# Block products for q and v in the attention layers of a four-layer graph network, with new step orders

## The chip, the cores and the metric

The kernel runs on one core of a Trainium2 chip. The metric is the device time of one execution in microseconds (us), as the median of several runs; lower is better.

## The reference

The input is x with 128 graphs of 64 nodes and 256 channels, 8192 rows in all, and one 64 x 64 adjacency matrix. Four layers follow one another, each with a residual:

```
h = relu(layernorm(x));  x = x + layer(h)
layer 0: normalized adjacency, two linear maps with batch norms
layer 1: two graph convolutions, then LSTMs over windows of 1 to 4 nodes
layer 2: q, k, v = split(h @ Wqkv); softmax(q k^T / 16 + adj, causal) v @ Wo
layer 3: q, k, v of 4 heads of 64 channels; softmax(q k^T / 8, masked where adj == 0) v
```

Everything is float32. This case is about layers 2 and 3. The kernel folds the weights of layer 2 beforehand: `wg0_sb` holds the product of the q and k weights, so that the scores are (h wg0) h^T and no k is computed, and `wg1_sb` holds the product of the v and output weights. So layer 2 has two projections of 256 x 256, layer 3 has three.

## The kernel before, in words

**Chunks.** The rows are cut into 16 chunks (`NCH`) of 512 rows (`CH`), four tiles (`NJ`) of 128 rows each. x stays in SBUF the whole time, one tile `xs[c]` a chunk. For a projection the kernel wants h with channels on the partitions (`hT`, two blocks `k` of 128 channels, 512 columns of rows). Most chunks get it by transposing 32 x 32 squares on VectorE, writing the result to DRAM (`put`) and reading it back with permuted rows (`get`, four transfers); a few use TensorE transposes (`chan2`, `chan3`).

**Attention as steps.** The part after the LSTMs is a list of small functions, the steps. Four order strings name them, with a chunk offset: `q2+0` is step q2 for the running chunk, `qa-2` is qa for the chunk two before. The order is written out by hand, and each engine executes its instructions of all steps in exactly this order. So a step that waits on an engine holds everything that is queued behind it there, on SP's queue of transfers too. FIRST opens the stage, THIRD does chunk 3, ROUND is the steady chunk, NORM a steady chunk that also prepares layer-2 input for chunks 14 and 15, LAST ends it. The offsets make the layers overlap: while chunk c is in layer 2, chunk c-2 has its layer-3 projections and chunk c-3 its last products.

The steps that the text speaks of:

- `load2`: reads hT of layer 2. `q2`, `copyq2`: q = two times two matmuls of 512 columns (`project_t`, L1526), copied from PSUM by ScalarE and VectorE. `v2a`, `v2b`: v, eight matmuls of 256 columns (`project_v`, L1519), two copies on ScalarE.
- `score2` (L1719): scores, then mask and maximum on VectorE, subtraction on GpSimd; `exp2` on ScalarE; `divide2` on VectorE; `turn2`: TensorE transposes (L1662); `out2` (L1750): product with v, added to x by VectorE (L1753).
- `keep`, `back`: write x to DRAM and read it in another order. `norm3a`, `norm3b`: statistics on VectorE, 1/sqrt on GpSimd. `apply3`: normalize and relu on ScalarE. `square3`: transposes on VectorE and the write. `load3`: the read.
- `sums_h` (GpSimd), `qa`, `q5`, `c11`, `q6`, `q3`, `c12`, `qc`, `qd`: q and k of layer 3 with seven block products (L1826), below. `v3a`, `v3b`: v of layer 3, as v2a and v2b. `q30`, `k30`, `q31`, `k31`: the plain projections, used for chunks 0 and 15 (before: for chunk 0 of the opening and the last chunk).
- `score3`, `exp3`, `sum3`, `divide3`, `turn3`, `out3` and `store`: the softmax of layer 3, its product and the write of the result. The last chunk has it in halves (`score3h`, `exp3a`, `turn3a`, `out3a`, `storea` and so on).
- `res1`, `pair1`: the layer-1 residual of chunks 14 and 15 and the reordering of their x, in the opening.

**Seven products.** A product of 2 x 2 blocks can be had with seven block products in place of eight, if sums of blocks are formed beforehand. For q and k of layer 3 the kernel does that: `sums_w` forms the sums of weight blocks once, `sums_h` the sums of blocks of hT for each chunk (four operations of 128 x 256 on GpSimd), `seven` issues the products into three PSUM banks X, Y, Z that go on accumulating, and copies (ScalarE) and adds (VectorE) take the four result blocks out at the right moments. X holds products 1, 6, 7 and 4 in turn, so that each has to wait until the sum before it has been read.

**PSUM.** In this stage eight banks are handed out in turn; the ninth request waits until the first bank has been read.

Of the kernel before, what the change touches and what calls it, by code (L numbers as in the profile page):

```python
# [13 lines left out]
P = 128  # L14
# [5 lines left out]
def kernel(  # L20
# [1508 lines left out]

    def begin_attention():  # L1530

        tiles = [shared(f"{n}2_0") for n in ("hT", "q")]
        for w, i in ((wg0_sb, 0), (wg1_sb, 1)):
            nc.sync.dma_start(w, products_far[:, :, i * D : (i + 1) * D])
        load2(0, tiles[0].rearrange("p (q n) -> p q n", q=Q))
        st[0, "q2"] = tiles[1].rearrange("p (k n) -> p k n", k=KD)
        st[0, "v2"] = wih1[0].rearrange("p g s f -> p (g s f)")[:, : NJ * D].rearrange("p (j d) -> p j d", d=D)
        yield
        for m in range(KD):
            nc.scalar.copy(st[0, "q2"][:, m, :], project_t(m, st[0, "hT2"], wg0_sb, "q2_0"))  # L1540
            yield
        for t in range(NJ // 2):
            project_v(st[0, "v2"], st[0, "hT2"], wg1_sb, 0, "2_0", [t])
            yield
        new_hT(last + 1)
        load2(1, hTs[last + 1][:, 1, :].rearrange("p (q n) -> p q n", q=Q))
        st[1, "q2"] = hTs[last + 1][:, 0, :].rearrange("p (k n) -> p k n", k=KD)
        yield
        for m in range(KD):
            nc.scalar.copy(st[1, "q2"][:, m, :], project_t(m, st[1, "hT2"], wg0_sb, "q2_1"))  # L1550
            yield
# [140 lines left out]

    @step
    def q2(c):
        st[c, "q2"] = q = l2.tile([P, KD, CH], F32, tag="q", name=f"q2_{c}")
        hT = st[c, "hT2"]
        nc.scalar.copy(q[:, 0, :], project_t(0, hT, wg0_sb, f"q2_{c}"))
        st[c, "q2b"] = project_t(1, hT, wg0_sb, f"q2_{c}")

    @step  # L1700
    def copyq2(c):
        nc.vector.tensor_copy(st[c, "q2"][:, 1, :], st.pop((c, "q2b")))

    def v2h(c, t):
        if not t:
            st[c, "v2"] = l2.tile([P, NJ, D], F32, tag="v", name=f"v2_{c}")
        project_v(st[c, "v2"], st[c, "hT2"], wg1_sb, 0, f"2_{c}", [t])

    steps["v2a"] = lambda c: v2h(c, 0)
    steps["v2b"] = lambda c: v2h(c, 1)  # L1710

    @step
    def score2(c):
        q, hT = st.pop((c, "q2")), st[c, "hT2"]
        ps = bank(f"s2_{c}")[:, : NJ * T].rearrange("p (j t) -> p j t", t=T)
        for j in range(NJ):
            for e in range(2):
                for k in range(KD):
                    nc.tensor.matmul(ps[half(e), j, :], q[:, k, columns(j, e)],  # L1719
                                     batch(hT, k, j, e), start=(k == 0), stop=(k == KD - 1))  # L1720
        st[c, "s2"] = s = l2.tile([P, NJ, T], F32, tag="s2", name=f"s2_{c}")
        nc.vector.scalar_tensor_tensor(s, ps, float(D) ** -0.5,
                                       mask2[:, None, :].to_broadcast([P, NJ, T]),
                                       op0=OP.mult, op1=OP.add)
        shifted(s, NJ, f"2_{c}")
# [52 lines left out]
    def qk3(c, m, k):  # L1778
        if not (m or k):
            for q in "qk":  # L1780
                st[c, q + "3"] = l2.tile([P, KD, CH], F32, tag=q, name=f"{q}3_{c}")
        ps = project_t(KD * k + m, st[c, "hT3"], w3_sb, f"{'qk'[k]}3_{c}")
        if m and k:
            nc.vector.tensor_copy(st[c, "k3"][:, m, :], ps)
        else:
            nc.scalar.copy(st[c, "qk"[k] + "3"][:, m, :], ps)
# [7 lines left out]
    l3 = []  # L1794

    @step
    def sums_w(c):
        ws3 = lasting.tile([P, 3 * 3 * P], F32, tag="wih1_3", name="ws3")[:, : 2 * 4 * P]
        l3.append(ws3.rearrange("p (i s f) -> p i s f", i=2, s=4))
        a = w3_sb[:, :, : 2 * D].rearrange("p k (i m f) -> p k m i f", i=2, m=KD)  # L1800
        d = l3[0].rearrange("p i s f -> p s i f")
        for dst, x, y, op in ((0, a[:, 0, 1], a[:, 1, 1], OP.add), (1, d[:, 0], a[:, 0, 0], OP.subtract),
                              (2, a[:, 0, 0], a[:, 0, 1], OP.subtract),
                              (3, a[:, 1, 0], d[:, 1], OP.subtract)):
            nc.gpsimd.tensor_tensor(d[:, dst], x, y, op)

    @step
    def sums_h(c):

        hT = st[c, "hT3"]  # L1810
        t = l3[1].tile([P, 4, CH // 2], F32, tag="td", name=f"td_{c}", bufs=1)
        t = [t[:, i, :].rearrange("p (a n) -> p a n", n=P) for i in range(4)]
        b = {(k, j): hT[:, k, 2 * j : 2 * j + 2, :] for k in range(KD) for j in range(2)}
        for f in differences(nc.gpsimd, t, b[0, 0], b[0, 1], b[1, 0], b[1, 1]):
            f()
        st[c, "o7"] = {1: b[0, 0], 2: b[1, 0], 3: b[1, 1], 4: t[3], 5: t[0], 6: t[1], 7: t[2]}

    def seven(c, kind, tag):
# [3 lines left out]
        for i in range(2):  # L1822
            m, k = {1: (0, 0), 2: (0, 1), 4: (1, 1)}.get(kind, (0, 0))
            w = (w3_sb[:, k, i * D + m * P : i * D + (m + 1) * P] if kind in (1, 2, 4) else
                 l3[0][:, i, {5: 0, 6: 1, 7: 2, 3: 3}[kind], :])
            nc.tensor.matmul(  # L1826
                st[c, tag][:, i * CH // 2 : (i + 1) * CH // 2].rearrange("p (a n) -> p a n", n=P), w,
                st[c, "o7"][kind], start=first and not i, stop=True, skip_group_check=True)
# [6 lines left out]

    @step
    def qa(c):
        st[c, "qk"] = l3[1].tile([P, 2, KD, CH], F32, tag="qk", name=f"qk_{c}", bufs=1)
# [4 lines left out]
    @step  # L1843
    def q5(c):
        seven(c, 5, "Y")
        nc.scalar.copy(part7(c, 1, 1), bank7(c, "Y"))
# [77 lines left out]

    def v3h(c, t):
        if not t:
            pool = l3[1] if l3[1:] else l2
            st[c, "v3"] = pool.tile([P, NJ, D], F32, tag="v", name=f"v3_{c}")
# [3 lines left out]
    steps["v3b"] = lambda c: v3h(c, 1)  # L1932

# [41 lines left out]
    def weights3(c):  # L1975
        nc.sync.dma_start(w3_sb, w3.rearrange("(k p) f -> p k f", p=P))

# [55 lines left out]
    def store(c, t):  # L2033
# [3 lines left out]
        for r in range(2):  # L2037
# [5 lines left out]
    ROUND = """exp3-3 q2+0 copyq2+0 sums_h-2 v2a+0 qa-2 v3a-2 sum3-3 load2+1 q6-2 score2+0 c11-2 q5-2 qc-2  # L2043
               exp2+0 back-2 load3-1 v2b+0 divide2+0 q3-2 turn2+0 qd-2 divide3-3 c12-2 out2+0 norm3a+0 norm3b+0
               turn3-3 v3b-2 out3-3 keep+0 score3-2 apply3+0 store-3 square3+0"""

    THIRD = """apply3-1 load2+1 v2a+0 score2+0 exp2+0 v2b+0 divide2+0 square3-1 load3-1 sums_h-2 qa-2 v3a-2
               turn3-3 turn2+0 q5-2 c11-2 out2+0 keep+0 norm3a+0 q6-2 q3-2 back-2 qc-2 norm3b+0 c12-2 v3b-2 qd-2
               apply3+0 out3-3 score3-2 store-3 square3+0"""

    NORM = """exp3-3 q2+0 copyq2+0 sums_h-2 v2a+0 qa-2 v3a-2 sum3-3 q6-2 score2+0 c11-2 q5-2 qc-2 exp2+0
              back-2 load3-1 v2b+0 norm2+1 divide2+0 q3-2 turn2+0 apply2+1 qd-2 divide3-3 c12-2 out2+0 norm3a+0
              norm3b+0 turn3-3 chan2+1 v3b-2 out3-3 keep+0 score3-2 apply3+0 store-3 square3+0"""

    FIRST = """load2+2 score2+0 exp2+0 v2a+1 v2b+1 divide2+0 score2+1 turn2+0 load2+3 v2a+2 exp2+1 res1+14
               out2+0 keep+0 weights3+0 q2+2 norm3+0 copyq2+2 divide2+1 v2b+2 apply3+0 back+0 score2+2 turn2+1
               chan3+0 out2+1 keep+1 exp2+2 sums_w+0 q30+0 k30+0 divide2+2 norm3+1 res1+15 res1+14 turn2+2
               q31+0 out2+2 keep+2 k31+0 apply3+1 res1+15 score3+0 square3+1 v3a+0 v3b+0 load3+1 exp3+0 q2+3  # L2060
               sum3+0 copyq2+3 divide3+0 norm3+2 res1+14 pair1+14 res1+15 pair1+15 pair1+14"""
    LAST = """exp3-2 sum3-2 load3+0 divide3-2 qa-1 q5-1 c11-1 v3a-1 q6-1 q3-1 c12-1 qc-1 turn3-2 qd-1 out3-2
              score3-1 q30+0 store-2 back-1 k30+0 back+0 exp3-1 q31+0 sum3-1 k31+0 divide3-1 score3h+0
              v3b-1 exp3a+0 sum3a+0 turn3-1 exp3b+0 v3a+0 divide3a+0 out3-1 sum3b+0 divide3b+0 store-1
              v3b+0 turn3a+0 turn3b+0 out3a+0 storea+0 out3b+0 storeb+0"""
# [7 lines left out]
    with tc.manual_schedule(engines={mybir.EngineType.PE, mybir.EngineType.DVE,  # L2073
# [3 lines left out]
        close_l1r()  # L2077
        pool3, close_l3 = pool("l3", 2, "right")
        l3.append(pool3)
        run(THIRD, SUP + 1)  # L2080
        run("pair1+15", 0)
        run(ROUND.replace("exp3-3 q2+0 copyq2+0", "q2+0 copyq2+0 exp3-3"), SUP + 2)
        for c in range(SUP + 3, NCH - SUP - 1):
            run(ROUND, c)
        for c in range(NCH - SUP - 1, NCH - 1):
            run(NORM, c)
        run(ROUND.replace("load2+1", "").replace("qd-2", "qd-2 sums_h-1"), NCH - 1)
        run(LAST, NCH - 1)
    close_l2()
    close_l3()  # L2090
# [48 lines left out]
```

## Time and profile before

| what | value |
|---|---|
| median of 3 runs | 1862.09 us (1861.8 to 1862.57) |
| profiled execution | 1861.38 us, its span 1859.6 us |
| TensorE clock granted | full |
| share of the span: PE, DVE, ACT, POOL | 98%, 71%, 56%, 33% |
| attention stage (first score2 to the end) | from 1490.06 to 1859.6 us |

PE is TensorE, PEld its weight loads, DVE VectorE, ACT ScalarE, POOL GpSimd, SP the engine that issues the transfers. A float32 matmul of the code is two MATMUL records in the profile. The profile leaves out digits in tile names: `hT<-far_n` is a read of load2, `hT<-far_h` one of load3, `x<-far_x` one of back. In a line of the timeline the first number is the start, the second the time until the last instruction of the group ends; ends of matmuls are modelled, so that neighbouring lines overlap, and the distance of two starts is the better measure of a price.

### The profile page before, as it was taken

The page shows a single profiled execution, that of the slowest core. Times are in us where ns is not written, and L with a number is a line of the kernel's source. Part 1 is how long each engine was busy: PE and PEld are TensorE (multiplying, and loading weights), DVE is VectorE, ACT ScalarE, POOL GpSimd, SP SyncE. Part 2 cuts the span into 40 slices and gives each one's busy share as a digit, 9 for nine tenths or more (in the row PEclk, how much of TensorE's full clock was granted, in tenths as well). Part 3 has the DMA queues.
Part 4 walks back from the last instruction along what each step waited for, and adds up shares of the span by engine and source line. Part 5 has one row for each costly group of instructions (what it writes and reads, how often), then busy time and mean ns, then how long its engine had stood idle before and what let it go on. Part 6 is the DMA issues. An engine that isn't in the chain of part 4 may idle for free.

```text
span 1859.6 us, 40656 instructions
## 1 busy us (share of the span) xinstructions
PE 1828.9 (98%) x15463; PEld 1509.7 (81%) x15463; DVE 1321.0 (71%) x3409; ACT 1050.3 (56%) x2498; POOL 614.2 (33%) x856
## 2 busy tenths in 40 slices
PE   9999999999999999999999999999999999999998
PEld 6877856996997898799699699789879867777775
DVE  6767857677667777777877776876667676666676
ACT  5766636556557556565665655746556634444453
POOL 5855723223214223322322322332222223222332
PEclk9999999999999999999999999999999999999999
DMA  3213652133433343242253443433244146555433
GB/s 116 71 62 142 228 212 68 53 111 125 156 118 125 114 159 141 79 153 84 114 159 115 148 146 127 148 114 126 102 120 148 36 152 190 147 146 146 126 115 103
DMA packets 113410, 234.48 MB, mean 126 GB/s; under 512 B 11712, under 2 KB 77120, under 8 KB 113216
## 3 DMA queue, kind: packets, MB, share of 16 engines
q1 hardware_dynamic: 112320, 230.02, 37.9%
q8 instruction: 123, 2.02, 0.5%
q0 software_dynamic: 320, 1.05, 0.2%
q10 hardware_dynamic: 576, 0.82, 0.1%
q14 instruction: 71, 0.58, 0.1%
HBM read 164.21 MB, written 67.63 MB: 125 GB/s over the span
## 4 chain that ended last, share of the span: by engine, by line
PE 88%; DVE 5%; ACT 2%; DMA 2%; POOL 1%; issue 1%; SPq 0%; DVEq 0%; ACTq 0%; POOLq 0%
PE x L1186 23%; PE z L1186 11%; PE y L1186 6%; PE v L1519 5%; PE y L1133 4%; PE x L1368 4%; PE y L1368 3%; PE p_q L1526 3%; PE u L948 3%; PE v L934 3%; PE x L1133 3%; PE X L1826 2%; PE X L436 2%; PE X L512 2%; PE z L1133 2%
## 5 line engine op out<-in xcount | busy, mean ns | idle before, releaser
L1101 ACT ACTIVATE l_gates<-l_gates,bias 128x256 f32<-128x256 f32 (+4 forms) x528 | 238.2, 498 | 210.9 <-DVE l_gates L1195 109.7
L1186 PE MATMUL x<-xd,wset 128*128 128x128 f32 (+2 forms) x1152 | 254.9, 303 | 0.8 <-ACT l_gates L1192 0.8
L1186 PE MATMUL x<-l_hd,wset 128*128 128x128 f32 (+2 forms) x1152 | 254.6, 303 | 0.0
L1252 POOL TENSOR_TENSOR l_gates<-l_gates 128x512 f32<-128x512 f32 (+2 forms) x48 | 75.3, 1568 | 368.5 <-ACT l_gates L1101 368.5
L1186 PEld LDWEIGHTS x<-xd,wset 128*128 128x128 f32 x1152 | 187.7, 191 | 6.4 <-issue 1.4
L1186 PEld LDWEIGHTS x<-l_hd,wset 128*128 128x128 f32 x1152 | 187.8, 191 | 5.0
L1195 DVE TENSOR_TENSOR l_gates<-l_gates,x 128x128 f32<-128x128 f32 (+2 forms) x384 | 121.1, 321 | 97.9 <-PE x L1186 95.2
L1195 DVE TENSOR_TENSOR l_gates<-l_gates,z 128x128 f32<-128x128 f32 (+2 forms) x384 | 102.4, 318 | 104.8 <-PE z L1186 102.8
L1186 PE MATMUL z<-l_hs,wset 128*128 128x128 f32 (+2 forms) x768 | 147.1, 304 | 0.7 <-DVE l_hs L1110 0.7
L1186 PE MATMUL z<-hT,wset 128*128 128x128 f32 (+2 forms) x768 | 146.2, 303 | 0.0
L1192 ACT COPY l_gates<-y 128x128 f32<-128x128 f32 (+2 forms) x192 | 53.2, 290 | 137.7 <-PE y L1186 131.5
L1186 PEld LDWEIGHTS z<-l_hs,wset 128*128 128x128 f32 x768 | 116.8, 191 | 5.8 <-DVE l_hs L1110 2.5
L1186 PEld LDWEIGHTS z<-hT,wset 128*128 128x128 f32 x768 | 117.1, 191 | 3.3
L1101 ACT ACTIVATE l_gates<-x,bias 128x128 f32<-128x128 f32 (+2 forms) x216 | 84.8, 393 | 28.6 <-PE x L1186 25.9
L1186 PE MATMUL x<-hT,wset 128*128 128x128 f32 (+2 forms) x384 | 85.8, 305 | 0.0
L1186 PE MATMUL x<-l_hs,wset 128*128 128x128 f32 (+2 forms) x384 | 84.9, 303 | 0.0
L327 POOL TENSOR_TENSOR xd<-hT 128x128 f32<-128x128 f32 (+2 forms) x72 | 42.2, 587 | 127.5 <-DVE hT L1112 113.8
L1186 PE MATMUL y<-l_hd,wset 128*128 128x128 f32 (+2 forms) x384 | 83.2, 309 | 0.0
L1643 POOL TENSOR_TENSOR s<-s,mx 128x256 f32<-128x256 f32 (+2 forms) x33 | 40.4, 1225 | 127.9 <-DVE mx L1642 96.5
L1186 PE MATMUL y<-xd,wset 128*128 128x128 f32 (+2 forms) x384 | 81.6, 304 | 0.0
L1267 ACT ACTIVATE l_gates<-l_cell 128x256 f32<-128x256 f32 (+2 forms) x144 | 55.2, 384 | 45.7 <-DVE l_cell L1266 45.2
L328 POOL TENSOR_TENSOR xd<-hT 128x128 f32<-128x128 f32 (+3 forms) x80 | 51.5, 644 | 67.0 <-DVE hT L1116 29.5
(356 smaller groups left out, 4564.5 us busy)
## 6 DMA issues: line engine op xcount, KB each, us to landing
wset<-wfar SPq DMA_DIRECT2D x96, 896.0 KB, 7.9
hT<-far_h SPq DMA_DIRECT2D x124, 128.0 KB, 4.6
far_h<-hm SPq DMA_DIRECT2D x16, 512.0 KB, 3.0
far_n<-xs SPq DMA_DIRECT2D x16, 512.0 KB, 2.9
xs<-far_n SPq DMA_DIRECT2D x64, 128.0 KB, 2.7
far_x<-xs SPq DMA_DIRECT2D x16, 512.0 KB, 2.7
x<-far_x SPq DMA_DIRECT2D x64, 128.0 KB, 3.7
xt<-in_x_dram SPq DMA_DIRECT2D x15, 512.0 KB, 3.8
```

Of the source, the lines that this page charges most:

```text
L934: nc.tensor.matmul(banks[m], wg0_sb[:, k, m * P : (m + 1) * P], agg[:, k, :], start=(k == 0), stop=(k == KD - 1))
L948: nc.tensor.matmul(banks[j // 2][:, j % 2, :], v[:, k, j * P : (j + 1) * P], wg1_sb[:, k, :], start=(k == 0), stop=(k == KD - 1))
L1101: nc.scalar.activation(gate(q, c, part), src, AF.Tanh if q == 2 else AF.Sigmoid, bias=bs[:, q * KD + c : q * KD + c + 1])
L1133: nc.tensor.matmul(folded(self.psum(kind)), wsets[p, self.q][:, BLOCKS[kind][0], :], ox[0][kind], start=kind in (1, 5), stop=True, skip_gr ...
L1186: nc.tensor.matmul(folded(self.psum(kind)), wsets[p, self.q][:, BLOCKS[kind][i], :], (ox[self.s] if part == "x" else oh)[kind], start=firs ...
L1192: nc.scalar.copy(gate(self.q, kind // 5, halves[kind // 5]), self.psum(kind))
L1195: nc.vector.tensor_add(gate(self.q, *dst), gate(self.q, *a), self.psum(kind))
L1252: nc.gpsimd.tensor_mul(gates[:, 0, :, :n], gates[:, 0, :, :n], gates[:, 2, :, :n])
L1267: nc.scalar.activation(gate(2, c, part), cells[:, c, part], AF.Tanh)
L1368: nc.tensor.matmul(folded(ps(g, kind)), single_block(KINDS1[kind])[:, g, :], right[kind], start=kind in (2, 5, 1), stop=True, skip_group_c ...
L1519: nc.tensor.matmul(ps[:, i, :], hT[:, k, j, :], w[:, k, first : first + D], start=(k == 0), stop=(k == KD - 1))
L1526: nc.tensor.matmul(ps.rearrange("p (a n) -> p a n", n=P), w[:, k, m * P : (m + 1) * P], hT[:, k], start=(k == 0), stop=(k == KD - 1))
```

## The change

q and v of layer 2 (chunks 4 to 15) and v of layer 3 (chunks 1 to 14) are computed with seven block products in place of eight. One set of layer-2 products makes q and v at once: `product_qv` issues for each kind one matmul of 256 columns for q, with the weight block as the stationary side, and two of 128 columns for v, with a block of hT as the stationary side, into one PSUM bank. Four copies of 512 columns (ScalarE) and three adds (VectorE) take the blocks out. `sums2` forms the block sums of hT on GpSimd for each chunk; `sums_g` and `sums_v` form those of the weights once. v of layer 3 works likewise with two banks (`va` to `v4`), with copies and adds of 256 columns.

```
def product_qv(c, kind, tag):
    ...
    nc.tensor.matmul(ps[:, : CH // 2].rearrange("p (a n) -> p a n", n=P), q, right, start=first,
                     stop=True, skip_group_check=True)
    for a in range(2):
        nc.tensor.matmul(ps[:, CH // 2 + a * P : CH // 2 + (a + 1) * P], right[:, a, :], v,
                         start=False, stop=True, skip_group_check=True)
...
def wz(c):
    need_qv(c)
    product_qv(c, 2, "Z")
    product_qv(c, 1, "X")
    copy2(c, 0, 0, "X")
# w5: product 5 into Y, copy; w11: add Z; w6: product 6 into X, copy; w3: product 3 into Y;
# w12: add Y; w7: product 7 into X, add; w4: product 4 into X, copy
...
def product_v3(c, kind, at, first=False):
    right = operand3(c, kind)
    w = block7(kind, lambda k, m: w3_sb[:, k, 2 * D + m * P : 2 * D + (m + 1) * P], l3["v"])
    for a in range(2):
        nc.tensor.matmul(at[:, a, :], right[:, a, :], w, start=first and not a, stop=True,
                         skip_group_check=True)
# va: products 2 and 1, copy; v5, v6: product and copy; v11, v12: adds; v3: product; v7: product, add;
# v4: product, copy
```

q and v of layer 2 now share one tile `qv` in two buffers, q stored by 128-row tiles, and score2 reads it so. The pool of layer 3 is opened earlier, by a step `change`. Products 1, 2 and 3 read hT itself and not the tile of sums.

The order strings are new throughout. FIRST takes the stage to chunk 3 of layer 2 and chunk 1 of layer 3 (it contains what THIRD did), ROUND runs for c = 4 to 11, and LAST runs everything after it in one list in which the steps of three or four chunks alternate; THIRD and NORM are gone. The diff of the orders, with LAST cut to its front and its end:

```
-    ROUND = """exp3-3 q2+0 copyq2+0 sums_h-2 v2a+0 qa-2 v3a-2 sum3-3 load2+1 q6-2 score2+0 c11-2 q5-2 qc-2
-               exp2+0 back-2 load3-1 v2b+0 divide2+0 q3-2 turn2+0 qd-2 divide3-3 c12-2 out2+0 norm3a+0 norm3b+0
-               turn3-3 v3b-2 out3-3 keep+0 score3-2 apply3+0 store-3 square3+0"""
-    FIRST = """load2+2 score2+0 exp2+0 v2a+1 v2b+1 divide2+0 score2+1 turn2+0 load2+3 v2a+2 exp2+1 res1+14
-               out2+0 keep+0 weights3+0 q2+2 ...
+    FIRST = """score2+0 exp2+0 divide2+0 score2+1 v2a+1 v2b+1 load2+2 res1+15 res1+14 turn2+0 exp2+1
+               res1+15 divide2+1 load2+4 v2a+2 out2+0 q2+2 norm3+0 copyq2+2 turn2+1 apply3+0 load2+3 v2b+2
+               out2+1 weights3+0 score2+2 res1+14 exp2+2 norm3+1 v2a+3 q2+3 divide2+2 chan3+0 apply3+1
+               res1+14 v2b+3 square3+1 turn2+2 res1+15 v3a+0 v3b+0 change+0 out2+2 sums_g+0 sums2+4 load3+1
+               q30+0 k30+0 sums_v+0 norm3+2 sums_h+1 copyq2+3 q31+0 k31+0 keep+0 score2+3 apply3+2 pair1+14
+               score3+0 wz+4 w5+4 sums_w+0 v5+1 exp2+3 w11+4 qa+1 q5+1 ...
+    ROUND = """out3-4 store-4 sums_h-2 exp3-3 out2-1 norm3a-1 norm3b-1 score2+0 sum3-3 wz+1 w5+1 qa-2 va-2
+               w6+1 load2+2 q6-2 exp2+0 q5-2 w11+1 v5-2 divide3-3 v11-2 keep-3 back-3 apply3-1 c11-2 qc-2
+               w7+1 v6-2 q3-2 divide2+0 w3+1 square3-1 w4+1 w12+1 qd-2 v7-2 sums2+2 c12-2 turn3-3 load3-1
+               v3-2 v4-2 v12-2 turn2+0 score3-2"""
+    LAST = """out3+8 keep+9 exp3+9 out2+11 score2+12 w5+13 keep+11 norm3a+11 store+8 sums_h+10 qa+10 sum3+9
+              norm3b+11 divide3+9 wz+13 q6+10 c11+10 exp2+12 w11+13 va+10 turn3+9 apply3+11 keep+10 ...
+              ... turn2+15 c11+13
+              c12+13 qc+13 out2+15 norm3a+15 v6+13 v3+13 v7+13 norm3b+15 qd+13 v4+13 load3+14 apply3+15
+              divide3+12 sums_h+14 score3+13 qa+14 turn3+12 square3+15 q5+14 c11+14 exp3+13 v11+13 q6+14
+              out3+12 sum3+13 back+13 load3+15 va+14 v5+14 q3+14 qc+14 v6+14 store+12 c12+14 v3+14 qd+14
+              v12+13 divide3+13 score3+14 v7+14 q30+15 keep+15 v12+14 exp3+14 back+15 k30+15 q31+15 sum3+14
+              k31+15 turn3+13 divide3+14 keep+14 score3h+15 exp3a+15 out3+13 sum3a+15 exp3b+15 divide3a+15
+              store+13 v3a+15 v3b+15 turn3a+15 turn3+14 back+14 v11+14 v4+14 sum3b+15 out3a+15 divide3b+15
+              storea+15 turn3b+15 out3+14 out3b+15 store+14 storeb+15"""
```

## The prediction

> **What bounds the kernel now.** I read four views of the kernel before. First the page's busy times, then the busy times of three stretches of the attention stage:
>
> ```profile
> PE 1828.9 (98%) x15463; PEld 1509.7 (81%) x15463; DVE 1321.0 (71%) x3409; ACT 1050.3 (56%) x2498; POOL 614.2 (33%) x856
> ...
> 1490.00:1560.00 70.00, 66.08 (x682) 45.57 (x680) 48.76 (x117) 31.23 (x62) 20.67 (x26) 1.00 0.59 182
> 1560.00:1760.00 200.00, 200.00 (x2434) 154.76 (x2432) 136.98 (x289) 89.26 (x162) 59.17 (x72) 1.00 0.53 145
> 1760.00:1860.00 100.00, 87.50 (x1178) 66.99 (x1178) 69.72 (x148) 42.30 (x78) 26.27 (x31) 0.99 0.34 105
> ```
>
> The columns are PE, PEld, DVE, ACT, POOL. In the middle TensorE never stops; it idles 3.9 us at the opening (70 - 66.08) and 12.5 us in the last 100 us, of which the tail after its last matmul is some 5.1. The whole stage starts at 1490.06 and holds 353.6 us of PE work. The timeline of PE in one steady chunk tells the price of each step by the distance of two starts (the durations overlap):
>
> ```profile
> 1692.12 1.20 PE L1719 MATMUL s<-hT,q 128*64 128x64 f32 x32
> ...
> 1702.62 1.16 PE L1956 MATMUL o<-v,att 64*64 64x64 f32 x64
> 1703.60 1.11 PE L1908 MATMUL s<-qk 64*64 64x64 f32 x64
> 1704.64 3.70 PE L1526 MATMUL p_q<-hT,wg_sb 128*128 128x512 f32 x8
> 1708.18 1.89 PE L1519 MATMUL v<-wg_sb,hT 128*128 128x256 f32 x8
> 1709.91 1.03 PE L1826 MATMUL Z<-hT,w_sb 128*128 128x256 f32 x4
> 1710.77 1.03 PE L1826 MATMUL X<-hT,w_sb 128*128 128x256 f32 x4
> ```
>
> A chunk takes 22.20 us (score2 starts at 1692.12 and again at 1714.32). One matmul in the code is two records ("passes"). A pass of 512 columns costs 3.54/8 = 0.4425 us, one of 256 columns 0.86/4 = 0.216. For 128 columns with a weight load each I take the LSTM stage:
>
> ```profile
> 1000.09 0.39 PE L1186 MATMUL x<-xd,wset 128*128 128x128 f32 x2
> 1000.31 0.39 PE L1186 MATMUL x<-l_hd,wset 128*128 128x128 f32 x2
> ```
>
> Two passes in 0.22: 0.111 us each. The end is set by a chain, not by PE (timeline, all engines):
>
> ```profile
> 1814.91 1.09 PE L1750 MATMUL o<-v,att 64*32 64x256 f32 x32
> ...
> 1826.55 0.33 SPq L261 DMA_DIRECT2D far_h<-mid  x1
> ...
> 1829.62 1.74 SPq L268 DMA_DIRECT2D hT<-far_h  x4
> ...
> 1835.87 1.98 PE L1526 MATMUL p_q<-hT,w_sb 128*128 128x512 f32 x4
> ...
> 1854.81 1.03 SPq L2039 DMA_DIRECT2D out_dram<-o  x2
> ```
>
> Between the last layer-2 output (ends 1815.93) and the first layer-3 projection of the same chunk lie 19.9 us: residual, norm, apply, transposes, a write of 512 KB, the read that waits for it (3.07 us after its issue), then 6.2 us to PE's start.
>
> **What the Trainium skill says.** "TensorE: Matmul & The Clock Gate", Back-to-back issue gap: the spacing of matmuls in a stream is set by the weight load and the matmul together. The trace agrees that a load per 128 columns can still be hidden: 0.111 us per pass although a load lasts 191 ns in the record. "VectorE: DVE Perf Modes", Why PSUM operands drop a tier: a float32 operand in PSUM leaves VectorE at its slowest rate. The trace agrees; the groups of instructions give one of the kernel's adds from PSUM 675 ns for 512 columns, and I price the new adds with it:
>
> ```profile
> L1850 DVE TENSOR_TENSOR qk<-qk,Z 128x512 f32<-128x512 f32 x14 | 9.5, 675 | 0.0
> ```
>  "Perfetto Trace Analysis", Optimization Strategy: find the gaps of the busiest engine and what blocks it there; the gaps of this trace, and those that the new orders make, are counted below.
>
> **The change part by part: PE's work.**
> 1. q and v of layer 2 for chunks 4 to 15 (wz to w4). Removed: q 8 x 0.4425 = 3.54, v 16 x 0.216 = 3.45. Added: 7 kinds x (2 passes of 256 + 4 of 128) = 7 x (0.432 + 0.444) = 6.13. Saved 0.86 x 12 chunks = 10.3.
> 2. v of layer 3 for chunks 1 to 14 (va to v4). Removed 3.45; added 7 x 4 x 0.111 = 3.11. Saved 0.34 x 14 = 4.8.
> 3. Order. In the old chunk three runs of matmuls on parts of the array (score2; out2; out3 with score3) stand apart, and each border costs about 0.09: the four passes before score2 take 0.955 and those after it 0.96 in place of 0.865. The new chunk puts score3, out3, out2 and score2 side by side: four borders fewer, 0.38. Eight chunks make 3.0, the rest of the stage I estimate at 0.8. Saved 3.8.
> Sum: 18.9 us, so a steady chunk is 22.2 - 0.86 - 0.34 - 0.38 = 20.6. Unknown here: changing between 256 and 128 columns 14 times a chunk. Bounds: nothing, or 0.04 each (what the row of eight transposes costs over 8 x 0.111), 0.56 a chunk, 6 us in all; I take nothing, because the eight passes of 256 columns that follow 512-column ones at 1708.18 take 1.73, 0.216 each, no more than the others.
>
> **Work put on other engines.** VectorE: three adds of 512 columns (0.68 each) and three of 256 (0.42) less one copy (0.66) come to 2.65 us a chunk. All its steady instructions by their row durations sum to 19.3 us a chunk; busy time runs some 11% below such sums (before: 16.7 by sum, 14.8 by the view), so some 17.1 of 20.6. Covered by PE, with about 3 us of slack. ScalarE: five copies of 0.58 go, four of 0.58 and four of 0.37 come, +0.9 on 9.9. GpSimd: four differences of 0.73 (sums2), +2.9 on 6.6; once, sums_g and sums_v, 12 operations on 128 columns at about 0.5, an estimate from the 0.73 of 256 columns. Their cover is the chunk's distance: sums2 runs one chunk ahead of w5. PSUM: 18 banks a chunk rotate in eight. Walking the order, each is given back before its turn: the closest are X and Y of the layer-2 products, and the bank of va, read by the copy of v4 some 1.3 us before out3 takes it. SP issues the same 15 transfers a chunk (four each for load2, back and load3, one each for keep, square3 and store).
>
> **Stalls.** Before, PE idles about 10.9 us inside the stage and 5.1 after its last matmul: 16.0.
> - Opening. The residual transfers of chunks 14 and 15 (res1) move ahead of load2 for chunks 4 and 3 on SP's queue. By the rows: score2 of chunk 1 is masked after the first divide, so VectorE's transposes for chunk 15 end near 1499.2; put; its read may start 3.07 later, 1502.3; three reads of four transfers, 1.8 us each, then about 3.6 to land: hT2_3 is there near 1511, while PE comes to v2a+3 near 1507.5. Stall 3.4; with the 0.5 before the first transposes and a wait of q5 for sums_w (GpSimd does the softmax subtraction first), 5.
> - Steady chunks: 0. The two waits of 1.46 in the old NORM chunks go.
> - Front of the long last order: VectorE has 110 us by row sums there against 107 of PE, so PE waits for divide3+9 (about 1.3) and similar places: 4 (1 to 6).
> - After out2+15: 15.3 us of PE work are queued ahead of q30+15. The chain: residual adds behind a VectorE backlog of about 1 (2.3), statistics 2.2 and one add 0.4 (5.0), rsqrt on GpSimd 1.5 (6.5), then on VectorE divide3+12, the masks and maximum of score3+13 (4), transposes 1.4: 12; write and read 8.8, less what the backlog lets go: 20. Stall 4.7. back+13 lies on SP between the write and the read, in the 3 us for which SP waits anyway.
> - The end: score3h+15 to turn3a+15 is covered by 4.5 us of matmuls, where the softmax half takes 5.3 (before: 5.6, covered by 6.8); turn3b+15 waits for a store and an add ahead of it on VectorE: together 1.9. The tail is 6.0, since 512 KB of chunk 14 leave just before the last 256 KB.
> Sum after: 5 + 0 + 4 + 4.7 + 1.9 + 6.0 = 21.6, 5.6 more than before.
>
> Net: -18.9 + 5.6 = -13.3. The profiled execution took 1861.38 (span 1859.6 and 1.8 around it), so 1848.1; the median of the runs shown lies 0.7 above it: **1849**.
>
> **Rivals.**
> - A, stalls no worse than before: the last order interleaves four chunks and hides the chain. Then -18.9: 1843; with 4 us of the old idle time gone too, 1839. For it: nothing in the steady part limits but PE. Against it: the chain after out2+15 can't be shorter than some 17 us (the old one less its 2.3 of waiting for VectorE), with 15.3 of cover.
> - B, VectorE becomes the bound: if its 19.3 us of row sums don't overlap as they did, and its waits add 10%, a chunk takes 21.2 to 21.8, and 5 to 9 us of the saving are lost: 1854 to 1858. For it: 110 against 107 in the last order. Against: about 3 us of slack.
> - C, slower: the 128-column passes don't run at 0.111, because here the activations are the stationary side and loads alternate with 256-column passes. There are 28 x 12 + 28 x 14 = 728 such passes; the change turns into a loss at 0.111 + 13.3/728 = 0.129 us, and at the 191 ns of a recorded weight load it costs 58 us: 1907. Against it: the LSTM stage runs 128-column passes with a load each at 0.111 for a thousand microseconds.
>
> **How the numbers follow.** Main case 0.47 (1845 to 1853), A 0.33, B 0.13, C 0.07. Left out of the range are C and the edge of A and B: 1839 to 1858. About 0.2% (3.7 us) is what a measurement of this kernel tells from no change: under 1858.4 is faster. Main, A and most of B: 0.90; the top of B and the smallest C: 0.04; the rest of C: 0.06.
>
> **What would show it.** Distance of score2 starts in the steady part 20.6 us with PE full (right), 21.2 and more with waits for VectorE (B); 128-column passes 0.111 apart (C if more); an idle stretch of about 3 us ahead of v2a+3 and of about 5 us ahead of q30+15, the latter ended by the read of hT3_15; the tail after the last matmul near 6 us. If PE has no waits in the last 100 us, A is right and my chain is mis-sized.

## The result and the profile after

| kernel | median (us) | range | ratio to before, with its 95% interval |
|---|---|---|---|
| before | 1862.01 | 1861.45 to 1863.61 (20 runs) | |
| changed | 1858.92 | 1856.35 to 1862.3 (20 runs) | 0.9983 [0.9976, 0.999] |

The gain is 3.1 us where 13 were forecast. The profiled execution took 1858.88, its span 1857.1. The page's busy times and the busy times of the three stretches, as shown of before:

```profile
PE 1816.6 (98%) x15847; PEld 1532.7 (83%) x15847; DVE 1350.6 (73%) x3475; ACT 1058.3 (57%) x2538; POOL 653.3 (35%) x916
...
1490.00:1560.00 70.00, 64.22 (x713) 47.72 (x712) 45.77 (x109) 28.49 (x58) 25.84 (x40) 0.95 0.51 142
1560.00:1760.00 200.00, 194.26 (x2724) 175.02 (x2723) 166.12 (x367) 100.17 (x201) 91.27 (x118) 0.99 0.49 152
1760.00:1860.00 100.00, 84.48 (x1247) 69.31 (x1246) 73.33 (x146) 42.44 (x84) 28.43 (x33) 0.97 0.39 125
```

TensorE's work in the stage (the first busy time, added over the three stretches) fell from 353.6 to 343.0, not to 334.7. Two things here were not in the forecast: the middle is no longer full (194.26 of 200), and the column behind the busy times, the granted clock, is 0.95 and 0.99 where it was 1.00.

An unstalled steady chunk, from the timeline of PE:

```profile
1599.93 1.20 PE L1836 MATMUL s<-hT,qv 128*64 128x64 f32 x32
...
1616.46 0.61 PE L2062 MATMUL w<-wsv,hT 128*128 128x128 f32 x4
1616.91 0.61 PE L2062 MATMUL v<-w_sb,td 128*128 128x128 f32 x4
1617.35 0.38 PE L1668 MATMUL tr<-ident,s 128*128 128x128 f32 x2
...
1620.71 1.20 PE L1836 MATMUL s<-hT,qv 128*64 128x64 f32 x32
```

It takes 20.78 us (20.6 forecast, 22.2 before), and four passes of 128 columns take 0.45 or 0.44: 0.111 each. So the price of a pass was right in the steady part. But the eight ROUND chunks together, from the score2 at 1557.77 to that at 1727.61, take 169.84, which is 3.6 more than 8 x 20.78. Of these, 2.45 are in stops like this one (timeline of PE; in brackets the idle time and its cause):

```profile
1703.71 1.08 PE L1867 MATMUL o<-qv,att 64*32 64x256 f32 x28
1706.27 0.62 PE L1867 MATMUL o<-qv,att 64*32 64x256 f32 x4 [1.48 <-issue]
```

"issue" means that the engine waited for nothing that the profile shows, here in the middle of one step's 32 equal matmuls. There are four such stops: 0.37 at 1579.5, 0.60 at 1642.1, 1.48 at 1704.8 and, in the last order, 2.07 at 1751.4. Each lies in or next to score2, in the row of small matmuls that the new orders put side by side.

The opening, again from the timeline of PE, and under it three stretches of it with the granted clock (third number from the end):

```profile
1506.92 1.20 PE L1836 MATMUL s<-hT,qv 128*64 128x64 f32 x32
1512.92 3.75 PE L1519 MATMUL v<-wg_sb,hT 128*128 128x256 f32 x8 [4.80 <-DMA hT<-far_n]
1516.46 4.42 PE L1526 MATMUL p_q<-hT,wg_sb 128*128 128x512 f32 x8
1520.71 1.04 PE L240 MATMUL tc_n<-ident,h 128*128 128x128 f32 x8
```
```profile
1508.00:1512.00 4.00, 0.12 (x5) 0.00 (x0) 3.83 (x13) 2.71 (x6) 0.69 (x2) 0.91 1.13 224
1512.00:1519.00 7.00, 6.08 (x13) 3.91 (x14) 0.74 (x3) 0.59 (x1) 6.68 (x14) 0.56 0.61 163
1519.00:1530.00 11.00, 11.00 (x76) 7.55 (x75) 6.26 (x14) 5.05 (x10) 2.36 (x5) 1.00 0.18 65
```

TensorE waits 4.80 us for hT2_3, and then the clock is half of full. The eight passes of v take 3.54 (1512.92 to 1516.46) in place of 1.73, the eight of q 4.25 in place of 3.54: behind the wait of 4.80 another 2.5 us are lost. The trace's record of the clock has it at 0.5 from 1511.3 to 1518.1, which is 6.8 us, and once more for 3.4 us after the stop of 2.07 at 1751, where 1.7 us are lost. In the trace of before, whose longest idle stretch in the stage is 1.82, the clock falls only after the last matmul.

The end, lines of PE, SP and VectorE from the timeline:

```profile
1808.54 1.09 PE L1867 MATMUL o<-qv,att 64*32 64x256 f32 x32
...
1829.96 1.95 PE L1526 MATMUL p_q<-hT,w_sb 128*128 128x512 f32 x4 [1.07 <-DMA hT<-far_h]
...
1845.86 2.98 SPq L279 DMA_DIRECT2D x<-far_x  x4
...
1851.20 1.28 DVE L2157 TENSOR_TENSOR o<-x,o 128x512 f32<-128x512 f32 x2 [2.53 <-DMA x<-far_x]
```

From the end of out2+15 (1809.57) to q30+15 are 20.4 us (20 forecast), but the wait at its end is only 1.07. After the last matmul (ends 1849.5) come 7.6 us: the last addition for chunk 14 waits for a read of x that SP issued only at 1845.86.

One execution each of the kernels of e11 and e12 below took over 6000 us (in the trace of the one of e12 TensorE is busy for 6076 us, the other engines about as long as elsewhere); both are left out, and that trace is not used.

### The profile page after: what moved, and what is told of

Same layout as the page of the kernel before. It is cut to its first block, busy times and chain, and to the rows that moved or that the text cites. A ratio compares the mean times of both kernels' runs of the same rounds, so it can differ in the third digit from the quotient of the medians.

```text
span 1857.1 us, 41626 instructions
## 1 busy us (share of the span) xinstructions
PE 1816.6 (98%) x15847; PEld 1532.7 (83%) x15847; DVE 1350.6 (73%) x3475; ACT 1058.3 (57%) x2538; POOL 653.3 (35%) x916
## 4 chain that ended last, share of the span: by engine, by line
PE 86%; DVE 6%; ACT 2%; issue 2%; POOL 2%; DMA 1%; SPq 1%; DVEq 0%; POOLq 0%; ACTq 0%
PE x L1186 22%; PE z L1186 11%; PE y L1186 6%; PE y L1133 4%; PE x L1368 4%; PE y L1368 3%; PE u L948 3%; PE v L934 3%; PE x L1133 3%; PE X L1938 2%; PE X L436 2%; PE X L512 2%; PE z L1133 2%; PE v L2062 1%; PE Y L1938 1%
## 5 line engine op out<-in xcount | busy, mean ns | idle before, releaser
L1110 DVE TENSOR_TENSOR l_hs<-l_gates 128x256 f32<-128x256 f32 (+4 forms) x120 | 51.4, 429 | 29.5 <-ACT l_gates L1159 13.8
```

## The experiments

In the labels, e7 and the kernels built on it (e9 to e14) have both the earlier reads of e1 and the new end of e4. Medians are compared with 1858.92 for the changed kernel and 1862 for before, whose median beside the runs of each experiment was 1861.8 to 1862.1.

**e1, the opening's reads first.** In FIRST:

```
-... load2+2 res1+15 res1+14 turn2+0 exp2+1 res1+15 divide2+1 load2+4 v2a+2 ... apply3+0 load2+3 v2b+2
+... load2+2 load2+4 load2+3 res1+15 res1+14 turn2+0 exp2+1 res1+15 divide2+1 v2a+2 ... apply3+0 v2b+2
```

> The changed kernel with load2 of chunks 4 and 3 placed ahead of the residual steps of chunks 15 and 14 in the opening; nothing else. Theory (transfer queue plus clock): the idle stretch of 4.8 us before the first v product of chunk 3 goes, and with it the stretch of about 7 us at half the TensorE clock that follows, which costs 3.0 us: together 6 to 8 us, so about 1852 against 1858.9 for the changed kernel. Rival (the stall only moves): the residual transfers become late instead and PE waits for them elsewhere: gain under 2 us. For the theory of instruction fetch the instruction stream of PE is unchanged, so the short idle stretches inside rows of small matmuls should lie at the same instructions as in the changed kernel (score2 after 25 of 32, and so on), whatever the transfers do.

Measured: 1852.01, ratio 0.9948 [0.9932, 0.9965], 6.9 faster. In the timeline of PE nothing stands between score2 and v2a+3:

```profile
1506.40 1.20 PE L1836 MATMUL s<-hT,qv 128*64 128x64 f32 x32
1507.53 2.00 PE L1519 MATMUL v<-wg_sb,hT 128*128 128x256 f32 x8
```

The clock of the stage stays at 1.00 up to the last matmul. From the start of that score2 to the transposes of L240 the changed kernel takes 13.8 us (1506.92 to 1520.71), this one 6.4 (1506.40 to 1512.79). So a wait of 4.8 us cost about 7. The stops marked issue stand at the same instructions as in the changed kernel, in the same four rows with 7, 21, 4 and 7 records still to come (there 7, 22, 4 and 8), though all of it now runs some 7 us earlier; their lengths are others (0.66, 1.17, 1.46 and 1.98).

**e2, the wait filled with work.** The same order, with 40 idle transposes (`keep_busy(40, "o")`) ahead of `v2a+3`: the reads stay where they are in the changed kernel, but TensorE doesn't idle.

> The changed kernel with 40 idle transposes (about 4.5 us of PE work that nobody reads) put on PE just ahead of the first v product of chunk 3, where PE waits 4.8 us for a transfer. Theory (the clock is halved because PE idled): the wait itself stays, but the granted clock stays at 1.00 and the next matmuls run at full pace: about 3 us faster than the changed kernel, 1856. Rival (the half clock has another cause, such as the load of the stage): the clock is halved as before and the time is the same or longer. The 40 instructions also shift the PE instruction stream against its fetch blocks: under the theory of instruction fetch the short idle stretches in the steady chunks move to other chunks or other places in the row.

Measured: 1852.06, ratio 0.9948 [0.9933, 0.9963], 6.9 faster, although 4.4 us of useless work went in. The clock is 1.00 in every stretch of the opening. That is more than the 2.5 of the clock. The rest, by the traces: v of chunk 3 starts 0.8 earlier (0.5 of it because the whole stage does), the stops marked issue fall from 4.5 to 1.4 (0.56, 0.49 and 0.37, in other chunks than before) while a new wait of 1.23 for VectorE comes, and with the stop of 2.07 its half-speed stretch of 1.7 is gone. That the stops had moved gave the hint followed in e9.

**e8, half as many transposes.** `keep_busy(20, "o")`.

> The changed kernel with 20 idle transposes ahead of v of chunk 3, where the second experiment had 40. They fill 2.2 of the 4.8 us, so TensorE still idles about 2.6 us there and the granted clock tells what length of idle halves it. If 2.6 us is enough, the clock falls to 0.5 once more and 1 to 3 us are lost as in the changed kernel; if not, it stays at 1.00 and the opening is as with 40. The stops of the steady part move once more, by 40 instructions against the changed kernel: their sum should lie between 2.6 and 4.5.

Measured: 1854.94, ratio 0.9962 [0.9948, 0.9975]. Timeline of PE, and one stretch of the busy times:

```profile
1513.00 3.54 PE L1519 MATMUL v<-wg_sb,hT 128*128 128x256 f32 x8 [2.26 <-DMA hT<-far_n]
```
```profile
1512.00:1517.00 5.00, 4.00 (x10) 3.11 (x11) 1.02 (x4) 0.37 (x1) 4.56 (x10) 0.66 0.90 237
```

2.26 us of idling halved the clock too: 0.34 x 5 = 1.7 us of clock lost, that is 3.4 us at 0.5. The stops marked issue sum to 3.2, as expected.

**e3, the row parted.** In ROUND, `wz+1` stands between `out2-1` and `score2+0`, and `v3-2` with `v12-2` behind `score3-2`, so that the four kinds of small matmuls are no longer side by side.

> The changed kernel with the steady order altered so that its four rows of small matmuls (score3, out3, out2, score2: 192 matmuls and as many weight loads within 4.2 us) are broken up: v3 stands between score3 and out3, the first two layer-2 products stand between out2 and score2. Theory (PE outruns its instruction fetch): the idle stretches inside these rows in the steady chunks (0.37, 0.61, 1.48 us in the changed kernel) go or fall below 0.3 us in total; against that, each additional border of such a row costs about 0.09 us, four a chunk, 2.9 us in eight chunks, so that the time stays within 2 us of the changed kernel. Rival (these stretches are waits for a semaphore or a bank that the profile does not name): they stay as long as before, and the time rises by about 3 us.

Measured: 1859.72 (1856.44 to 1862.57, 16 runs), ratio 0.9987 [0.9979, 0.9994], no gain. The stops in ROUND fall only from 2.45 to 1.84 (1.15 and 0.69, in other chunks), and an unstalled chunk takes 21.33 in place of 20.78: the extra borders between kinds of matmul cost 0.55 in each of eight chunks. That these 4.4 us made no greater loss fits the clock, which in this trace was halved for 3.4 us in all and not 10. In this kernel, parting every row cost more than it gave.

**e4, the end of chunk 14.** `keep+14` and `back+14` move ahead of the last chunk's products, and x of chunk 14 gets a buffer that is free by then:

```
-... score3+14 v7+14 q30+15 keep+15 v12+14 exp3+14 back+15 ... divide3+14 keep+14 ... turn3+14 back+14 v11+14
+... score3+14 v7+14 keep+14 q30+15 keep+15 v12+14 exp3+14 back+14 back+15 ... divide3+14 ... turn3+14 v11+14
```

> The changed kernel with the read of chunk 14's x (back) issued before the store of chunk 13, into another buffer (the tile that held the normalized rows), and its write (keep) earlier too. Theory (the tail waits for this read): VectorE no longer waits 2.5 us for it before the last stores, and the time falls by about 2.5 us, to 1856.4. Rival (the tail is set by the store transfers themselves): the time is the same within 0.5 us.

Measured: 1855.62, ratio 0.9967 [0.9954, 0.998], 3.3 faster. The tail is 6.1 in place of 7.6; the addition starts 0.5 after VectorE's last work, and its releaser is a product:

```profile
1846.52 1.29 DVE L2157 TENSOR_TENSOR o<-x,o 128x512 f32<-128x512 f32 x2 [0.51 <-PE o L2142]
```

The other 1.8 are not seen in the tail: in this trace the half-speed stretch of the opening lasted 3.4 us, not 6.8, and the stop at 1751 was 1.5 with no half clock after it. Whether the edit or chance shortened them, one trace doesn't tell.

**e7, both.**

> The changed kernel with both the earlier reads of chunks 4 and 3 (first experiment) and the rearranged end of chunk 14 (fourth). If the two losses are separate, the gains add: 6.9 from the opening and 1.5 (tail alone, 7.6 to 6.1) to 3.3 (all that the fourth gained), so 1848.7 to 1850.5. If the gain of the fourth was partly a shorter spell of halved clock in the opening, which the first removes already, the sum stays at the upper end, 1850.5. Either way it is faster than both kernels.

Measured: 1849.06 (1847.85 to 1850.38), ratio 0.993 [0.9918, 0.9943]: 9.9 faster than the changed kernel and 13 faster than before. That is inside the expected 1848.7 to 1850.5; with an interval of some 2 us to either side it doesn't tell which of e4's gains remain beside e1's.

**e9, the instruction stream shifted.** e7 with the 40 transposes of e2, at a place where nothing waits.

> The kernel with the earlier reads and the rearranged end, plus 40 idle transposes (80 instructions of TensorE with their weight loads, 4.4 us at 0.111) ahead of v of chunk 3, where nothing waits any more. Theory: the short stops marked issue in the rows of small matmuls come from instruction packets of 256 instructions that arrive late, so they depend on the place of a packet's border in the stream; 80 instructions move them to the places that the second experiment showed (about 1.2, 0.6, 0.5 and 0.4 us, 2.7 in all, in place of 0.7, 1.2, 1.5 and 2.0, 5.3 in all), so it is 1.8 us slower than without the transposes. Rival: the stops belong to the rows themselves or to a wait that the profile doesn't show; then they stay where they are and the loss is 4.4 us.

Measured: 1850.38, ratio 0.9936 [0.9924, 0.9949], only 1.3 slower, with 4.4 us more work. The stops of e7 (1.27, 1.09, 0.76, 1.48 and 1.91, at 1549, 1574, 1637, 1700 and 1747) are gone, and two others stand at 1618.9 and 1681.9, where e2 had them at 1618.8 and 1681.8. From the timelines of PE, first the row with the longest stop in e7, then, of e9, a wait, one of the two new stops and the row that had the longest:

```profile
1745.73 0.97 PE L1836 MATMUL s<-hT,qv 128*64 128x64 f32 x25
1748.62 0.46 PE L1836 MATMUL s<-hT,qv 128*64 128x64 f32 x7 [1.91 <-issue]
```
```profile
1556.62 0.70 PE L1773 MATMUL Z<-hT,wg_sb 128*128 128x256 f32 x2 [1.83 <-DVE xs L1870]
...
1619.42 0.69 PE L1836 MATMUL s<-hT,qv 128*64 128x64 f32 x14 [0.58 <-issue]
...
1747.30 1.20 PE L1836 MATMUL s<-hT,qv 128*64 128x64 f32 x32
```

There all 32 records of score2 run through. The sizes: 6.5 us of stops in e7; in e9 0.58 and 1.04, and 1.83 at the start of the first ROUND for which the profile names a VectorE addition, 3.45 in all. The difference, 3.1, is what the transposes cost less than their 4.4. So a stop belongs to a place in TensorE's instruction stream and not to a step.

What lies at such places the page of the changed kernel tells in its part on the queues (queue, kind: packets, MB, share):

```profile
q8 instruction: 126, 2.06, 0.5%
```

That is 16 KB each. The trace of the changed kernel holds 32225 instructions of TensorE (15847 matmuls, as many weight loads, and its semaphore instructions), 256 per packet; in the kernels with fewer instructions there are fewer packets (124 in e10, 123 in before), again 256 or 257 each. If TensorE's instructions are counted in order in each of the fifteen traces used, all 49 stops of the stage marked issue and longer than 0.2 us stand at the 193rd or 194th of a run of 256, and each ends 1.2 to 1.7 us after a packet has landed. The waits for other engines and for transfers stand anywhere in the 256. Seven waits that the profile puts down to another instruction stand at that place too (194 or 195), with the same distance from a packet: the 1.83 above and the 1.23 of e2 are among them. So the stops are at borders between packets, and with those seven they are waits for instructions as far as a trace can tell; there is no record of the wait itself. Most borders pass without a stop (33 of 37 in the stage of the changed kernel).

**e5 and e6, one part of the change undone, under the new orders.** In e5 `va` and `v4` are the old `v3a` and `v3b`, and the other v steps are empty. In e6 `wz`, `w6`, `w7` are the old projections of q and v, and the other w steps and `sums2` are empty.

> The changed kernel with v of the third layer computed by plain projections again, under the new orders. By the prediction's price the block products save 0.34 us in each of 14 chunks, 4.8 us, so this is 4.8 slower than the changed kernel, 1863.7. If the short stops in the rows of small matmuls take part of that back (the row of small matmuls stays, but a chunk has 12 to 13 matmul instructions fewer), the loss is smaller: 2 to 4. If VectorE or the waits limited the changed kernel, this one is no slower.

> The changed kernel with q and v of the second layer of all chunks computed by plain projections again, under the new orders. By the prediction's price the block products save 0.86 us in each of 12 chunks, 10.3 us, so this is 10.3 slower than the changed kernel, 1869.2. A smaller loss, 5 to 8, would say that the products cost more than the sum of their passes (changes of width, or waits for VectorE and GpSimd), or that stops went with them.

Measured: e5 1857.02, ratio 0.9974 [0.9965, 0.9984], that is 1.9 **faster** than with the block products, where 4.8 slower was expected; e6 1861.78, ratio 0.9998 [0.999, 1.0007], 2.9 slower, where 10.3 was expected. Ahead of their last matmul both traces have 3.4 us at half clock, where the changed kernel's has 10, so these two comparisons mix in the clock. The same two edits on e7, where the clock stays full:

**e10 and e11.**

> The kernel with the earlier reads and the rearranged end, with v of the third layer by plain projections. Under the old opening the plain form was 1.9 us faster than the block products, although its TensorE work was 3.9 longer (by the busy windows, less what the halved clock took), because it lost less to stops and to the halved clock. Without the idle stretch of the opening, theory: the block products' 3.9 less work remains, the stops differ by some 2 us in the other direction, so the plain form is 1 to 3 us slower than 1849.1. Rival: the block products of v3 don't pay in any surroundings, and the plain form is again about 2 us faster, 1847.

> The kernel with the earlier reads and the rearranged end, with q and v of the second layer by plain projections. The unstalled steady chunk was 0.74 longer in the plain form under the old opening (21.52 against 20.78), and the whole only 2.9 longer. If the halved clock and the stops hid the rest, the loss is now 0.74 x 12 = 8.9 less some 3 us of stops, about 6: 1855. If the block products themselves are worth only 3, 1852.

Measured: e10 1848.29 (1847.82 to 1849.34), ratio 0.9925 [0.9912, 0.9937], 0.8 faster than e7 (the ranges overlap), where 1 to 3 slower was expected; e11 1853.7, ratio 0.9951 [0.9938, 0.9965], 4.6 slower, where 6 was expected. TensorE's time and its idle time in three parts, added up from the starts in the timelines:

| part, us of work + idle | e7, all block products | e10, plain v of layer 3 | e11, plain q and v of layer 2 |
|---|---|---|---|
| first score2 to that of chunk 4 | 58.88 + 2.26 | 58.95 + 1.42 | 59.43 + 1.82 |
| eight chunks of ROUND | 167.65 + 3.32 | 170.57 + 2.23 | 173.74 + 1.82 |
| the last order | 111.97 + 7.50 | 111.96 + 5.26 | 113.10 + 4.56 |

In ROUND the products give what they should: 2.92 / 8 = 0.37 a chunk for v of layer 3 and 6.09 / 8 = 0.76 for q and v of layer 2. In the last order v of layer 3 (five chunks) gives nothing, q and v of layer 2 (three chunks) 1.1. By line, v of layer 3 takes 17.7 us there for 140 passes, 0.1265 each, against 0.1114 in ROUND; the plain projections take 17.8 for 80. And the idle time is 4.2 longer with v in block products than without, 4.9 longer with q and v than without. The stops at the borders between packets explain the first wholly and most of the second: they sum to 6.5 in e7, 2.2 in e10 and 3.0 in e11 (in each of the last two, one of them is put down to TensorE itself).

**e12, e13 and e14, the row with the longest stop parted.** `qa+11` moves between `score3+10` and `score2+13`:

```
-out3+9 w12+13 sums_h+11 apply3+12 back+10 score3+10 back+9 score2+13 qa+11 v3+10 norm2+15
+out3+9 w12+13 sums_h+11 apply3+12 back+10 score3+10 back+9 qa+11 score2+13 v3+10 norm2+15
```

e12 and e14 are e7 with this move, e13 is e10 with it.

> The kernel with the earlier reads and the rearranged end, and in the last order the first products of q and k of chunk 11 (qa, eight passes of 256 columns, 1.73 us) moved between score3 of chunk 10 and score2 of chunk 13, which stand side by side there and hold the longest stop, 1.91 us marked issue. Theory of late instruction packets: the eight slower passes give the packet 1.7 us more time, so the stop shrinks by 1.5 or more, one border costs 0.14, gain about 1.5: 1847.6. Rival: the stop belongs to score2 of chunk 13 itself, for which something late is needed; then it moves with it and only the part covered by qa goes, or nothing changes.

> The kernel with the earlier reads, the rearranged end and v of the third layer by plain projections (1848.3), and qa of chunk 11 moved between score3 of chunk 10 and score2 of chunk 13. In this stream no stop lies in that row (its longest are 0.8, elsewhere). Theory of late instruction packets: the move then costs only a border, 0.1 to 0.3 us, and the time is 1848.5. Rival: the move helped by its order (q and k of chunk 11 earlier), not by the stop; then it gains here too what it gained with the block products, 1.2 us: 1847.1.

> The kernel with the earlier reads, the rearranged end and the moved qa, v of the third layer in block products (median 1847.85). Its trace is to show where the 1.2 us came from. Theory: in the row of out3 of chunk 9, score3 of chunk 10, qa and score2 of chunk 13 the stop of 1.91 marked issue is below 0.4, and the other stops (1.1, 0.8, 1.5) stand where they were. Rival: the stop is still there and another wait has gone.

Measured: e12 1847.4, ratio 0.9918 [0.9905, 0.9932]; e14, the same kernel, 1847.76 (1846.45 to 1849.04), ratio 0.9925 [0.9912, 0.9939], 1.3 faster than e7; e13 1849.62 (1848.75 to 1850.4), ratio 0.9934 [0.9921, 0.9946]. The row in the timeline of e14:

```profile
1743.07 1.11 PE L2025 MATMUL s<-qk 64*64 64x64 f32 x64
1744.11 1.13 PE L1938 MATMUL Z<-hT,w_sb 128*128 128x256 f32 x4
1745.08 1.03 PE L1938 MATMUL X<-hT,w_sb 128*128 128x256 f32 x4
1746.04 1.20 PE L1836 MATMUL s<-hT,qv 128*64 128x64 f32 x32
```

No stop is left in it; those of 1.3 and 1.5 at 1549 and 1698 stand where they were, and those of 1.1 and 0.8, which the edit doesn't touch, are 0.5 and 0.2 in this execution. Where the row held no stop, the same move gained nothing and cost 1.3 (0.4 by the spans of the profiled executions). So the traces speak for the stop and not the order; the medians alone, whose ranges overlap with those of e7 and e10, would not settle it. This kernel is the fastest found, 14 us under before; e10 lies 0.5 above it, within the ranges.

## Why the prediction was wrong, step by step

The forecast for the profiled span was 1846.3 (1848.1 less 1.8); it was 1857.1. The 10.8 us divide so:

| term | forecast | measured | difference |
|---|---|---|---|
| start of the stage | 1490.06 | 1490.76 | 0.7 |
| TensorE's work at full clock (from the first score2 on 342.2, less 4.2) | 334.7 | 338.0 | 3.3 |
| half clock after idling | not there | 2.5 + 1.7 | 4.2 |
| idle inside the stage | 5 + 0 + 10.6 | 5.8 + 2.5 + 8.3 | 1.0 |
| tail | 6.0 | 7.6 | 1.6 |

That the idle time comes out near the forecast is luck: the opening and the stops were 5.3 longer than forecast (2.07 of the 8.3 is a stop), and the rest of the last order idled 4.4 less.

1. **Stall of the opening.** Place and cause were right (v2a+3, the read of hT2_3 behind the residual's reads), its size 4.8, not 3.4: the last read was issued some 0.9 later than forecast, and the data landed some 4.3 after it and not 3.6. The failed step is the price: the idle time was put in at its length. e1 shows the true bill, about 7, and e2 that filling the wait saves the half clock. The Trainium skill, "TensorE: Matmul & The Clock Gate", Part 1: The HAM clock gate, describes this: the default state of the array's clock is throttled to half, and an idle window of some 3.4 us brings it back. The prediction used the same page for the spacing of matmuls and not for this. The runs agree with the window: stretches of 3.4 and 6.8 us at 0.5. They don't agree that a whole window must be idle: 2.26 us were enough in e8, and 2.07 in the changed kernel.

2. **"Steady chunks: 0."** Wrong, the second failed step: 2.5 us of stops in ROUND and 2.07 in the last order, with another 1.7 of half clock behind that one. The prediction took the borders that fall away as pure gain (0.38 a chunk). It didn't ask what the row of four groups of small matmuls asks of the instruction supply: 192 matmuls and 192 weight loads in 4.2 us, about 90 instructions per us, one and a half packets. Before had two such stops, of 0.87 and 1.35, inside score3, which I passed over. That the stops go with the place in the stream (e9, e2), stand at the borders between packets and end shortly after one has landed is shown; so is that the stop of 1.91 is not there when the row is parted at it (e14). That the packet was late is the reading that fits all of this; no trace records such a wait.

3. **TensorE's price.** 128-column passes at 0.111, and changing between 256 and 128 columns at nothing: both right in ROUND. The timeline of PE, behind the score2 at 1599.93:

```profile
1601.06 0.70 PE L1773 MATMUL Z<-hT,wg_sb 128*128 128x256 f32 x2
1601.60 0.61 PE L1776 MATMUL Z<-wg_sb,hT 128*128 128x128 f32 x4
1602.04 0.60 PE L1773 MATMUL X<-hT,wg_sb 128*128 128x256 f32 x2
1602.47 0.61 PE L1776 MATMUL X<-wg_sb,hT 128*128 128x128 f32 x4
```

The pairs of 256 columns take 0.43 (0.216 or 0.217 a pass), also behind 128-column passes; only the first, behind score2, takes 0.54. This border, 0.10, is why q and v save 0.76 a chunk and not 0.86: in e11 the 512-column passes that stand behind score2 take 0.442 each and show no border. The mis-sized term is the last order, which was priced like ROUND: v of layer 3 in five chunks saves nothing there (1.7 forecast), q and v of layer 2 in three chunks 1.1 (2.6 forecast). Passes of 128 columns take up to 0.178 there behind rows of small matmuls. Over the stage the saving was 7.8 for q and v of layer 2 (10.3 forecast) and 3.0 for v of layer 3 (4.8); the rest of the 15.6 saved, 4.8, is the order's (3.8 forecast). Rival C's turning point was 0.129; in the last order v is at 0.1265.

4. **The chain after out2+15.** Its 20 us were right (20.4). The wait was 1.07 and not 4.7, since the work queued ahead of q30+15 took 17.6 and not 15.3, with 1.7 of other waits in it. The last order idled 8.3 against 10.6, in spite of the stop of 2.07.

5. **The tail.** "512 KB of chunk 14 leave just before the last 256 KB" was right, but the read of x for chunk 14 was left out of the walk: back+14 stands behind store+13 on SP, and its data came at 1851.1. e4 took this away.

6. **VectorE and GpSimd.** Right: 139.7 us busy in 1560 to 1730 make 17.1 for a chunk of 20.78 (17.1 forecast), and GpSimd has 9.2 (9.5). No wait of ROUND for VectorE in the changed kernel exceeds 0.25, so rival B falls; that the time fell near its range is chance. Rival A fell with the opening alone. The price of the adds held (0.66 to 0.69 for 512 columns). But the 675 ns don't show that the operand in PSUM makes an add slow: multiplications of 512 columns that read SBUF alone (L1110 of before) take 692.

The spread of the changed kernel, 6 us where before has 2, goes with the clock: five executions with a mean clock of 0.998 average 1857.7, seven with 0.995 or 0.996 average 1860.4.

What stays open: why some borders between packets stop TensorE and most don't, and what sets the length (the stop in score2 of chunk 8, at the same instruction each time, was 0.2 in e14, 0.6 in the changed kernel and 1.2 in e1); why single products cost more in the last order beyond their borders; and which of two idle stretches of about 2 us is followed by half clock.

## What to carry to other kernels

In these traces an idle stretch of TensorE of about 2 us or more costs its length and up to one or two spells of 3.4 us at half clock behind it, each up to 1.7 us of work; work in place of it (an earlier read, or even useless transposes) can pay more than the stall. Small matmuls set side by side save borders but need some 90 instructions per us, so look for stops marked issue in such rows (and for waits put down to another engine that stand at the same place in the instruction count), and part the row that has one. A price per pass from a steady row holds in steady rows; where single products are scattered among other shapes, take the border into the price, and walk every read on the queue of transfers up to the last addition.

## What the runs showed of the hardware

- The granted clock was halved for 3.4 or 6.8 us after idle stretches of 4.80, 2.26 and 2.07 us. It was not after 1.91 (e7), 1.98 (e1) and 2.12 (e6), so some 2 us decide, and not the length alone. After 4.41 to 4.60 (e3 to e6) it was halved for 3.4 us each time.
- TensorE stopped for 0.2 to 2.1 us in or just behind rows of small matmuls (one of 49 elsewhere), without a wait that the profile shows, only at every 256th of its instructions, and went on 1.2 to 1.7 us after an instruction packet of 16 KB had landed. The places moved when 80 instructions were put in 40 us or more ahead.
- A border of about 0.1 us shows between a row of small matmuls and passes of 256 columns, and none before passes of 512.
- 40 idle transposes made the kernel 6.9 us faster.
